# Row fetching in a recommender kernel: SyncE takes a tile of rows every 5.35 steps instead of every 5.5, ScalarE one tile more

## The chip, the cores and the metric

The kernel runs on one core of a Trainium2 chip. The metric is the time on the device in microseconds (us), the median of the timed runs. One further execution is recorded by the hardware profiler; every row of the profile comes from it. The engines are named as the profile names them: PE (TensorE, with its weight loads as PEld), DVE (VectorE), ACT (ScalarE), POOL (GpSimd) and SP (SyncE). ACT and SP also issue transfers on DMA queues of their own, written ACTq and SPq.

## The reference

For each of 16384 examples there are 69 user ids and one label id. Each id picks a row of 96 floats from a table of 100001 rows. Every user row is weighted by a small attention network that sees it beside the label's row; the weighted rows are summed in 10 groups, and a network of three layers follows.

```
u   = emb[batch_user]                       # 16384 x 69 x 96
ql  = emb[batch_label[:, 0]]
z   = concatenate([q, u, q - u, q * u])     # q is ql for all 69
h   = dice(z @ W1 + b1, a1)                 # 64 wide
att = (h @ W2 + b2) @ W3 + b3
pre = where(batch_user < ITEM_NUM, u * att, 0)
pooled = einsum('gf,bfe->bge', window, pre) # 10 groups
x   = concatenate([pooled, ql])
x   = dice(bn(x @ Wf1 + bf1), af1)          # 200 wide
x   = dice(bn(x @ Wf2 + bf2), af2)          # 80 wide
return x @ Wf3 + bf3
```

The bulk of the memory work is the lookup of 16384 x 69 = 1130496 rows of 384 bytes, that is, 8832 tiles of 128 rows. A row is put on each of 128 partitions.

## The kernel before

The examples are cut into 32 blocks of 512. A block has 69 chunks of 512 looked-up rows, and a chunk has four tiles of 128 rows. Two chunks together are a pair, which is the work of one step: 1104 steps (NPAIR) in all, eight tiles each.

Each tile's rows come in one of three ways. Most are gathered by POOL, with one indirect DMA per tile (`gather`, L265 and L266) into a buffer `u` of which there are 15. Some are fetched by SP, row by row: one DMA of 384 bytes for each row, at an address that SP has first loaded into a register (class `Singles`: `load` with L286, `fetch` with L301). The rest are fetched in the same way by ACT. Only the last of the four tiles of a chunk (SLOT = 3) can be fetched row by row. The lists SP_CHUNKS and ACT_CHUNKS (L52, L55) say in which chunks. SP has the odd chunks, so the second chunk of a pair; its tile number s lies in step int(5.5 s) + 6, 199 tiles in all. ACT has even chunks; its tile number s lies in step (s + 1) * 128 // 20 + 2, 170 tiles in all. That leaves 8832 - 199 - 170 = 8463 gathers for POOL, and 128 more for the label rows (`head_gather`).

The rows that SP and ACT fetch land in `ring`, twelve buffers of 128 rows: eight for SP, four for ACT. PE waits on a semaphore before it reads one (`wait_for_single`, L318), and a tile that reuses a buffer waits until PE has finished with the tile that was in it.

In a step PE transposes the eight tiles (`fetch`, L359, through `read_rows`, L325), DVE copies the transposed rows and multiplies them with the label's, PE forms the hidden layer (`hidden`), ACT and DVE apply its activation, PE makes the attention weights (`attend_rows`, `spread`), and seven steps after the fetch (POOL_LAG) PE multiplies the same rows again with the weights to pool them (`pool`, also L325 through `read_rows`). The three layers on top of a finished block (`top1`, `top2`, `top3`) are spread over later steps.

The order on every engine is written out by hand in `plan`, a list of work for each step. SP's tile is planned six steps ahead of its use (L598 and L599); on SP itself there is nothing else but a few loads of ids, one every four blocks (`load_ids`, planned 50 steps ahead of their first use), and the stores of the result at the end. ACT's rows are planned 20 per step (`scalar_rows`, L610), behind the activations of the step, so ACT's queue holds both in one order. Behind the waiting transpose of a fetched tile stands all further work of PE.

Of the kernel before, what the change touches and what calls it, by code (L numbers as in the profile page):

```python
# [18 lines left out]
P = 128  # L19
# [29 lines left out]

ROW_BYTES = 4 * E  # L50
SLOT = 3
SP_CHUNKS = [2 * (int(5.5 * s) + 6) + 1 for s in range(199)]  # L52
SP_RING = 8
ACT_ROWS = 20
ACT_CHUNKS = [2 * ((s + 1) * P // ACT_ROWS + 2) for s in range(170)]  # L55
ACT_RING = 4
SINGLES = SP_CHUNKS + ACT_CHUNKS
NSB = (len(SINGLES) + P - 1) // P
# [57 lines left out]
def rec_kernel(  # L116
# [477 lines left out]
    def at(step, *work):  # L594
        plan.setdefault(step, []).extend(work)

    by_sync = Singles("sp", nc.sync, mybir.EngineType.SP, SP_CHUNKS, 0, range(SP_RING), 32)
    for s, m in enumerate(SP_CHUNKS):  # L598
        at(max(0, m // 2 - 6), lambda s=s: by_sync.fetch(s, 0, P))  # L599
# [4 lines left out]
        mybir.EngineType.Activation,  # L604
        ACT_CHUNKS,
        len(SP_CHUNKS),
        range(SP_RING, SP_RING + ACT_RING),
        32,
    )
    def scalar_rows(i):  # L610

        row, stop = i * ACT_ROWS, min((i + 1) * ACT_ROWS, len(ACT_CHUNKS) * P)
        while row < stop:
# [140 lines left out]
```

## Time and profile before

| | us |
|---|---|
| timed runs, median of 3 (lowest, highest) | 16757.55 (16755.94, 16759.19) |
| the profiled execution's own time | 10782.2 |
| its span, first to last instruction | 10780.4 |
| PE busy, mean granted clock 0.749 | 8756.9 |
| POOL busy | 8110.8 |
| DVE busy | 4235.1 |
| ACT busy | 1884.4 |

The profiled execution is 5975 us shorter than the timed runs. Every row of the profile therefore describes an execution of 10782 us, and what the timed runs do in the rest is not in it.

How to read it: a group's row names the line, the engine, the operation and the tiles (output, then inputs), the count, the busy time in us and the mean of one in ns, and after the second bar the idle time of the engine just before such instructions and what ended it. "issue" means that nothing which the profile shows was waited for. Instructions that only issue a DMA, load a register or wait on a semaphore are not counted as busy: SP, which does nothing else, has no share at all, and ACT's share leaves out its row fetching. In a view of one tile the three numbers of a row are the shortest, median and longest duration in ns, then the first and last start in us.

### The profile page before, as it was taken

What the parts mean: (1) busy time and instruction counts of PE and PEld (TensorE: products, weight loads), DVE (VectorE), ACT (ScalarE), POOL (GpSimd) and SP (SyncE); (2) the same over time, 40 slices, a digit from 0 to 9 for tenths busy, and PEclk for the clock granted to TensorE, in tenths of its full rate; (3) what the DMA queues carried; (4) which work ended last, traced back from release to release, by engine and by line L of the source; (5) the groups of instructions that cost most, each with busy time, mean ns of one, the idle gap of its engine ahead of it and who ended that gap; (6) DMA issues with size and microseconds to landing.
All of it is one profiled execution on the core that took longest, in us unless ns stands there. A gap on an engine that the chain in (4) does not pass through costs nothing.

```text
span 10780.4 us, 204439 instructions
## 1 busy us (share of the span) xinstructions
PE 8756.9 (81%) x41797; PEld 4310.8 (40%) x41797; DVE 4235.1 (39%) x7535; ACT 1884.4 (17%) x2761; POOL 8110.8 (75%) x8597
## 2 busy tenths in 40 slices
PE   6888888888887788877888788888887887888888
PEld 3434444434433344433433344333343343443335
DVE  4333333333333333333333343333333334333333
ACT  1111111111111111111111111111111111111112
POOL 7777777777777777777777777777777777777776
PEclk7777777677777777777777777777777777777778
DMA  2222222222222222222222222222222222222221
GB/s 50 42 42 42 45 42 42 42 42 45 42 42 42 45 42 42 42 42 45 42 42 42 42 44 42 42 42 42 44 42 42 42 42 44 42 42 42 42 42 34
DMA packets 372495, 460.70 MB, mean 43 GB/s; under 512 B 232114, under 2 KB 232626, under 8 KB 371106
## 3 DMA queue, kind: packets, MB, share of 16 engines
q0 software_dynamic: 274912, 422.81, 18.9%
q1 hardware_dynamic: 52802, 16.36, 1.0%
q10 hardware_dynamic: 43520, 8.44, 0.7%
q14 instruction: 925, 7.58, 0.2%
q8 instruction: 336, 5.51, 0.2%
HBM read 446.81 MB, written 0.07 MB: 41 GB/s over the span
## 4 chain that ended last, share of the span: by engine, by line
POOL 40%; PE 21%; issue 19%; DMA 12%; ACTq 6%; ACT 2%; DVE 1%; POOLq 0%
POOL u L266 40%; DMA u<-in_rows,ids 12%; ACTq L301 4%; PE acc L325 4%; PE p L502 4%; PE ph L399 3%; PE ph L403 3%; PE ptr L325 2%; PE prow L414 1%; ACTq L286 1%; PE pa L423 1%; ACT y L405 1%; POOL q L266 1%; PE ph L396 1%; PE ph L401 1%
## 5 line engine op out<-in xcount | busy, mean ns | idle before, releaser
L266 POOL DMA_INDIRECT u<-in_rows,ids x8463 | 7989.1, 944 | 2583.5 <-issue 2389.6
L325 PE MATMUL ptr<-ident,u 128*96 128x128 f32 x8463 | 1925.1, 332 | 1606.1 <-DMA u<-in_rows,ids 1555.6
L407 DVE TENSOR_TENSOR y<-ph,y 128x512 f32<-128x512 f32 x1104 | 763.5, 692 | 4972.6 <-ACT y L406 4699.0
L325 PEld LDWEIGHTS acc<-rw,u 128*96 128x96 f32 x15702 | 1674.4, 188 | 1332.5 <-issue 840.4
L325 PEld LDWEIGHTS ptr<-ident,u 128*96 128x96 f32 x8463 | 1131.6, 151 | 2282.7 <-DMA u<-in_rows,ids 1853.2
L325 PE MATMUL acc<-rw,u 128*96 128x20 f32 x15702 | 1792.0, 259 | 212.0 <-DVE rw L436 177.6
L376 DVE COPY uT<-ptr 96x512 f32<-96x512 f32 x2208 | 1489.0, 674 | 739.9 <-PE ptr L325 737.5
L405 ACT ACTIVATE y<-ph 128x512 f32<-128x512 f32 x1104 | 658.8, 597 | 6119.1 <-PE ph L403 3304.1
L399 PE MATMUL ph<-uT,A 128*64 128x512 f32 x4096 | 1598.9, 856 | 0.0
L403 PE MATMUL ph<-quT,wn 96*64 96x512 f32 x4416 | 1540.5, 767 | 0.0
L379 DVE TENSOR_TENSOR quT<-ptr,qT 96x512 f32<-96x512 f32 x2048 | 1379.1, 673 | 0.0
L406 ACT ACTIVATE y<-y,wn,na1c 128x512 f32<-128x512 f32 x1104 | 897.9, 813 | 36.6
L403 PEld LDWEIGHTS ph<-quT,wn 96*64 96x64 f32 x4416 | 429.4, 183 | 1002.5 <-issue 1001.8
L502 PE MATMUL p<-pooled,wf 96*100 96x512 f32 (+1 forms) x1400 | 667.7, 624 | 0.0
L414 PE MATMUL prow<-y,v 128*32 128x512 f32 x2208 | 507.2, 885 | 65.4 <-DVE y L407 57.6
L399 PEld LDWEIGHTS ph<-uT,A 128*64 128x64 f32 x4096 | 259.6, 172 | 609.6 <-issue 605.5
L416 ACT COPY row<-prow 128x512 f32<-128x512 f32 (+1 forms) x277 | 161.6, 583 | 1733.2 <-issue 675.0
L470 DVE COPY pooled<-acc 96x160 f32<-96x160 f32 x1008 | 420.5, 417 | 99.1 <-PE acc L325 97.6
L502 PE MATMUL p<-pre,V 96*100 96x512 f32 (+1 forms) x700 | 398.0, 714 | 11.1 <-DVE x L485 10.8
L502 PEld LDWEIGHTS p<-pooled,wf 96*100 96x100 f32 x1400 | 249.6, 190 | 316.5 <-issue 316.5
L436 DVE SCALAR_TENSOR_TENSOR rw<-patt,bb,wn 128x320 f32<-128x320 f32 x554 | 276.1, 539 | 116.8 <-PE patt L431 114.7
L485 DVE SCALAR_TENSOR_TENSOR x<-p,wf,g 100x512 f32<-100x512 f32 (+3 forms) x105 | 73.9, 704 | 523.6 <-ACT g L484 523.5
(72 smaller groups left out, 2706.1 us busy)
## 6 DMA issues: line engine op xcount, KB each, us to landing
ring<-in_rows SPq DMA_DIRECT2D x25472, 0.4 KB
ring<-in_rows ACTq DMA_DIRECT2D x21760, 0.4 KB
u<-in_rows,ids POOLq DMA_INDIRECT x8463
ids<-in_idx SPq DMA_DIRECT2D x8, 560.0 KB, 3.9
q<-in_emb,ids POOLq DMA_INDIRECT x128
wf<-in_far SPq DMA_DIRECT2D x1, 1209.0 KB, 8.3
wn<-in_near SPq DMA_DIRECT2D x1, 236.0 KB, 3.4
offsets<-in_single_rows SPq DMA_DIRECT2D x1, 192.0 KB, 2.5
```

What stands on the lines that cost most here:

```text
L266: nc.gpsimd.indirect_dma_start(out=dst, out_offset=None, in_=table, in_offset=bass.IndirectOffsetOnAxis(ap=index, axis=0),)
L301: d = self.engine.dma_start(out=ring[r : r + 1, b], in_=row_bytes[:, bass.ds(self.values[r], ROW_BYTES)]).then_inc(self.sems[k], 16)
L325: ins = op(out, ring[:, at[0]].bitcast(F32) if at else u[:, 4 * (c % 2) + t, :], other, **how)
L376: nc.vector.tensor_copy(uT[j][0:E], ptr)
L379: nc.vector.tensor_tensor(quT[:, j, :].rearrange("e (s f) -> e s f", f=FM), ptr.rearrange("e (s f) -> e s f", f=FM), by_field(q[:, k * NS ...
L399: nc.tensor.matmul(p, As[n % 2][:, k // 4, :], uT[j], start=True, stop=False)
L403: nc.tensor.matmul(p, Wp, quT[:, j, :], start=False, stop=True)
L405: nc.scalar.activation(y, ph, AF.Sigmoid, scale=S_DICE)
L406: nc.scalar.activation(y, y, AF.Identity, bias=a1c, scale=na1c)
L407: nc.vector.tensor_mul(y, ph, y)
L414: nc.tensor.matmul(pr[32 * k : 32 * (k + 1), :], v2, ys[b + k], start=True, stop=True)
L502: nc.tensor.matmul(p1, w[:, h * DH : (h + 1) * DH], x, start=(k == 0), stop=(k == KTOP - 1))
```

## The change

Two numbers change in each of two lists. SP's tile number s now lies in step int(5.35 s) + 6, and there are 204 of them in place of 199. ACT's list keeps its spacing and has one tile more at its end, number 170, in step 1096. What is in these lists is no longer gathered by POOL. The buffers, the lead of six steps, ACT's 20 rows per step and all other work stay as they are.

```diff
-SP_CHUNKS = [2 * (int(5.5 * s) + 6) + 1 for s in range(199)]
+SP_CHUNKS = [2 * (int(5.35 * s) + 6) + 1 for s in range(204)]
 SP_RING = 8
 ACT_ROWS = 20
-ACT_CHUNKS = [2 * ((s + 1) * P // ACT_ROWS + 2) for s in range(170)]
+ACT_CHUNKS = [2 * ((s + 1) * P // ACT_ROWS + 2) for s in range(171)]
 ACT_RING = 4
```

## The prediction

> **What bounds the kernel now.** I read the page first, busy time and chain, because it says whether the engine that the change relieves sets the time.
>
> ```profile
> PE 8756.9 (81%) x41797; PEld 4310.8 (40%) x41797; DVE 4235.1 (39%) x7535; ACT 1884.4 (17%) x2761; POOL 8110.8 (75%) x8597
> POOL u L266 40%; DMA u<-in_rows,ids 12%; ACTq L301 4%; PE acc L325 4%; PE p L502 4%; PE ph L399 3%; PE ph L403 3%; PE ptr L325 2%; PE prow L414 1%; ACTq L286 1%; PE pa L423 1%; ACT y L405 1%; POOL q L266 1%; PE ph L396 1%; PE ph L401 1%
> L266 POOL DMA_INDIRECT u<-in_rows,ids x8463 | 7989.1, 944 | 2583.5 <-issue 2389.6
> ```
>
> PE is busiest by share, yet the chain runs mostly through POOL's gathers (L266), and the idle time ahead of a gather is "issue": nothing was being waited for. So next the timeline of POOL in mid-kernel and at its end, and the gathers' busy time in four equal stretches.
>
> ```profile
> 5002.83 0.94 POOL L266 DMA_INDIRECT u<-in_rows,ids  x1 [0.30 <-issue]
> 5004.08 0.94 POOL L266 DMA_INDIRECT u<-in_rows,ids  x1 [0.30 <-issue]
> ...
> 10733.37 0.94 POOL L266 DMA_INDIRECT u<-in_rows,ids  x1 [0.30 <-issue]
> 10734.61 0.95 POOL L266 DMA_INDIRECT u<-in_rows,ids  x1 [0.30 <-issue]
> ```
>
> ```profile
> 1000.00:3000.00 2000.00, 1511.23 (x1602) 0.74 0.21 43
> 3000.00:5000.00 2000.00, 1511.19 (x1602) 0.75 0.21 43
> 5000.00:7000.00 2000.00, 1510.95 (x1603) 0.76 0.21 43
> 7000.00:9000.00 2000.00, 1511.23 (x1602) 0.75 0.21 43
> ```
>
> The columns are the stretch, its length, POOL's busy time and count, the clock, the DMA share and GB/s. The reader should see one gather every 2000 / 1602 = 1.248 us, alike in all stretches. 8463 gathers of users and 128 of labels make 8591; 8591 x 1.249 = 10730 us, and the first starts at 3.2 us, so the last should end near 10734; it ends at 10735.6. POOL is never held up. The profiled span is those 10736 us and a tail of 45 us.
>
> Two other queues fetch rows one by one. Their limits come from the view of the row buffer (tile ring), the row loads, the waits of SP's queue, and the timelines of SP and PE.
>
> ```profile
> L301 SPq DMA_DIRECT2D ring<-in_rows x25472: 227/228/482, 6.7 to 10349.8; - x199
> L301 ACTq DMA_DIRECT2D ring<-in_rows x21760: 213/214/587, 18.6 to 10606.0; - x200
> L286 SPq TENSOR_LOAD <-offsets x796: 2025/2176/2410, 4.5 to 10337.5; - x199
> ...
> SPq L301 <- PE ptr L325: 84.8, 36, 13.2
> SPq L301 <- PE acc L325: 27.5, 7, 10.9
> SPq L301 <- PE ph L403: 0.9, 4, 0.3
> ...
> 6.74 48.92 SPq L301 DMA_DIRECT2D ring<-in_rows  x128
> 79.65 0.27 PE L325 MATMUL ptr<-ident,ring 128*96 128x128 f32 x1
> 10677.94 0.42 PE L325 MATMUL ptr<-ident,ring 128*96 128x128 f32 x1
> ```
>
> SP is nearly full too. From 6.7 to 10349.8 us it waits only 113 us for a free buffer. Taking off the waits and the 49 us of the last tile leaves (10343.1 - 113.2 - 49) / 198 = 51.4 us per tile. The kernel takes 10780 / 1104 = 9.76 us per step, so 5.5 steps are 53.7 us. SP issues its first tile by 55.7 us and PE reads it at 79.65: a lead of 24 us. The last is issued by 10350 and read at 10678: a lead of 328 us. SP gains about 2 us per tile until the eight buffers stop it; the waits are that stop.
>
> **What the skill's pages say.** Perfetto Trace Analysis, section Identifying the Most-Contended Engine, takes the engine with the highest occupancy, for GPSIMD the occupancy percentage. By it POOL would have a quarter of its time free. The trace disagrees: the 0.30 us after each gather come back every time with no wait behind them. The forecast goes by the period, 1.249 us. DMA: Bandwidth & Descriptors, section Why a DMA increments its semaphore by 16 and not by 1, says that a transfer with one row uses one engine, the lowest-numbered, on SP and ACT alike. All single rows would then share one DMA engine. The profile gives their two queues 1.0% and 0.7% of sixteen engines, at most 27% of one; with 18.9% for the gathers that engine is under half busy, so 768 further rows (1.6% of 47232) should not slow it. The trace does not name the engine.
>
> **The change, part by part.** SP: 204 tiles for 199, so 5 more tiles, 640 more rows, 20 more loads of offsets. ACT: one more tile, 128 rows and 4 loads. POOL: 8463 - 5 - 1 = 8457 gathers. PE, DVE and the ACT activations keep their counts; a transpose or a pooling product reads the ring instead of a gathered tile (239 ns for either, in the groups of pooling products).
>
> POOL, on the path: 6 x 1.249 = 7.5 us less. The tail after the last gather is PE's chain and keeps its 45 us.
>
> SP, off the path: five tiles are 5 x 51.4 = 257 us more issuing, hidden while the lead is positive. One tile per 5.35 steps is needed every 5.35 x 9.76 = 52.2 us against 51.4: a margin of 0.8 us, where it was 2.3. The dangerous place is the start. Tile 2 moves from step 17 to step 16, whose fourth transposes begin at 176.4 us before the change, and SP is done with it at 55.7 + 2 x 51.3 = 158.3: a lead of 18 us. The landing takes about 1 us more. Step by step with the old step times this is the smallest lead. The last tile, 203, is at step 1092; SP finishes it near 55.7 + 203 x 51.4 = 10490 us and PE wants it near 10646, 156 us later. With such leads SP never reaches the buffer limit, so the 113 us of waits should vanish; those waits cost nothing now. The ids loads, queued between tiles on SP, are planned 50 steps (some 490 us) ahead and stay early. If the cover fails, PE stands before its transpose (wait_for_single), and behind it stand all later PE work, the release of gather buffers and then POOL: each us short per tile costs about a us per tile.
>
> ACT, on the path only near the end: its 20 rows per step and the loads stay as they were, but go on for 6.4 steps longer, steps 1088 to 1094, with the tile read at step 1096. That is 128 x 0.32 + 4 x 2.27 = 50 us of ACT's queue, the 0.32 us being the spacing of rows that are not held up (20 in 6.37 us at 5016 us), in steps of 62 us that also hold activations of the last blocks. ACT does this all through the kernel with POOL unhindered. Bounds: nothing while POOL's 15 buffers absorb it, 50 us if all of it were exposed; I take nothing. No gain can come from it. A ring read instead of a gathered one could spare PE some of its 3488 us of waiting on gathers, but PE does not set the end; bounded by 0 and the 7.5 us that POOL grants.
>
> Sum against the profiled execution: 10782.2 - 7.5 = 10774.7 us, -0.07%.
>
> **Against the median.** The timed runs are 16757.55 us, 5975 us longer than the profiled execution, and no view shows where. They spread by 3 us in 16757, so whatever adds it is as regular as POOL's gathers. If the gathers set those runs too, a period is (16757.5 - 48) / 8591 = 1.945 us and six are 11.7 us; if the excess is something apart, the gain stays 7.5 us. I take the first, an estimate: 16757.6 - 11.7 = 16745.9. Both are within 0.2%, about what a measurement of this kernel can tell from no change.
>
> **The rivals.**
> No gain: in the timed runs PE or the excess sets the time and POOL has slack. For it: PE is busy 81%, and its clock is 0.75. Against: the profile's unbroken row of gathers. 16757.
> SP becomes the limit (slower). Its place is the wait before the ring transpose; it decides when a tile costs SP more than 5.35 steps. In the profile that needs 0.8 us more per tile. In the timed runs a step is 16757.55 / 1104 = 15.18 us: if the excess sits in the rows that SP issues, a tile takes 5.5 x 15.18 = 83.5 us, five more are 418 us, and three more steps follow the last tile, 3 x 9.76 = 29 us: 17204. For it: SP is the second fullest resource, and one step period fits as well as another. Against: rows are issued here with leads up to 328 us.
> A smaller loss: rows share a DMA engine or ACT's last tile shows. 768 rows beside 47232 + 8591 x 8 rows on one engine are +0.6%, 16860 if that engine sets the timed runs; ACT's tile gives at most 50 us, some 78 us at 15.18 us per step: 16824. Against: the queues' low shares.
> Faster: the timed runs hold a disturbance that a different spacing of SP's rows removes in part; then anywhere from 16700 down to the profile's 10775. Nothing in the trace speaks for it but the gap itself.
>
> **How the numbers follow.** The likeliest, gathers set the pace, 0.62 (its own range 16725 to 16775); no gain 0.08; smaller loss 0.08; SP the limit 0.15; faster by over 0.2% 0.07. Same is 0.62 + 0.08 = 0.70, slower 0.23, faster 0.07. The range reaches from 16690, taking in the small gains, to 16870, taking in the smaller losses; it leaves out SP as the limit and the large gains, about 0.19.
>
> **What would show it.** 8457 gathers of users at 944 ns with 0.30 us of issue between them, some 1602 per 2000 us; a span near 10773; SP with 26112 rows, hardly a wait for PE, its last row near 10490 us; PE reading SP's last tile about 150 us later; ACT's rows ending some 60 us later than 10606. I am wrong if PE waits ahead of ring transposes, gaps open between POOL's gathers, SP's tile takes over 52 us, or the timed runs move where the profile does not: then the excess of 5975 us lies in the rows and not in the gathers.

## The result and the profile after

The changed kernel takes 17020.54 us (median of 4 runs, 17013.28 to 17026.13), the kernel before 16758.37: 1.57% slower, ratio 1.0157 with a 95% interval of 1.0145 to 1.0169. The forecast was 16746, within 16690 to 16870.

On two of the four chips that the experiments met, the kernel before takes some 16760 us every time, and on the other two some 10782 us every time. (One of the long chips was met on two occasions, the other three on one each.) The one profile that the prediction had was of the second sort, and all its timed runs were of the first. Below these are called the long chips and the short chips, and only runs of the same sort are compared.

The page of the changed kernel's profile, on a long chip: the busy line, the chain, and the groups of gathers and of ring transposes.

```profile
PE 8944.0 (53%) x41797; PEld 4580.1 (27%) x41797; DVE 4209.5 (25%) x7535; ACT 1882.8 (11%) x2761; POOL 8101.4 (48%) x8591
SPq 62%; issue 36%; PE 1%; ACTq 0%; DMA 0%; ACT 0%; DVE 0%; POOL 0%; another core or an unknown queue 0%
SPq L301 54%; SPq L286 8%; ACTq L301 0%; PE p L502 0%; PE acc L325 0%; DMA ring<-in_rows 0%; PE ph L399 0%; PE ptr L325 0%; PE ph L403 0%; PE patt L431 0%; POOL u L266 0%; ACTq L286 0%; ACT y L405 0%; PE prow L414 0%
L266 POOL DMA_INDIRECT u<-in_rows,ids x8457 | 7979.6, 944 | 8774.5 <-PE ptr L325 3354.8
L325 PE MATMUL ptr<-ident,ring 128*96 128x128 f32 x375 | 139.4, 372 | 4411.4 <-DMA ring<-in_rows 4343.0
```

A gather still takes 944 ns and POOL's work is the same, but POOL now stands idle for 8774.5 us. The chain is SP's queue from end to end: 62% for SP's instructions and 36% for the time between them in which nothing was waited for. PE waits 4343 us for rows that SP fetches (the idle time in the last row). No engine's share of busy time would have pointed there, as SP has none.

The gathers in four stretches of the changed kernel (columns as in the prediction: 1602 per stretch had been the full row), and SP's timeline over some 100 us, of the changed kernel and of the first profile of the kernel before, on a short chip:

```profile
1000.00:3000.00 2000.00, 947.31 (x1004) 0.67 0.14 27
3000.00:5000.00 2000.00, 960.51 (x1018) 0.67 0.14 27
5000.00:7000.00 2000.00, 966.12 (x1024) 0.67 0.14 27
7000.00:9000.00 2000.00, 947.33 (x1004) 0.68 0.14 27
```

```profile
5000.18 99.74 SPq L301 DMA_DIRECT2D ring<-in_rows  x161
3999.88 109.75 SPq L301 DMA_DIRECT2D ring<-in_rows  x277
```

The changed kernel's SP issues 161 rows in 99.74 us, 0.62 us a row. In the first profile of the kernel before it issued 277 in 109.75 us, 0.40 us a row. SP does not wait for a free buffer meanwhile: in its own list of waits nothing but 1.4 us is left under L301. It just issues more slowly.

### The profile page after: what moved, and what is told of

It reads as the page before. It is cut to its first block, busy times and chain, and to the rows that moved or that the text cites. A ratio compares the mean times of both kernels' runs of the same rounds, so it can differ in the third digit from the quotient of the medians.

```text
span 17013.7 us, 205998 instructions
## 1 busy us (share of the span) xinstructions
PE 8944.0 (53%) x41797; PEld 4580.1 (27%) x41797; DVE 4209.5 (25%) x7535; ACT 1882.8 (11%) x2761; POOL 8101.4 (48%) x8591
## 4 chain that ended last, share of the span: by engine, by line
SPq 62%; issue 36%; PE 1%; ACTq 0%; DMA 0%; ACT 0%; DVE 0%; POOL 0%; another core or an unknown queue 0%
SPq L301 54%; SPq L286 8%; ACTq L301 0%; PE p L502 0%; PE acc L325 0%; DMA ring<-in_rows 0%; PE ph L399 0%; PE ptr L325 0%; PE ph L403 0%; PE patt L431 0%; POOL u L266 0%; ACTq L286 0%; ACT y L405 0%; PE prow L414 0%
## 5 line engine op out<-in xcount | busy, mean ns | idle before, releaser
L266 POOL DMA_INDIRECT u<-in_rows,ids x8457 | 7979.6, 944 | 8774.5 <-PE ptr L325 3354.8
L325 PE MATMUL acc<-rw,u 128*96 128x20 f32 x15688 | 1915.1, 268 | 1155.8 <-issue 491.4
L325 PE MATMUL ptr<-ident,ring 128*96 128x128 f32 x375 | 139.4, 372 | 4411.4 <-DMA ring<-in_rows 4343.0
L325 PEld LDWEIGHTS acc<-rw,u 128*96 128x96 f32 x15688 | 1795.3, 199 | 2268.1 <-issue 1296.3
L325 PE MATMUL ptr<-ident,u 128*96 128x128 f32 x8457 | 1518.8, 330 | 451.9 <-issue 358.5
L325 PEld LDWEIGHTS ptr<-ident,u 128*96 128x96 f32 x8457 | 1188.1, 161 | 605.3 <-issue 528.5
L325 PEld LDWEIGHTS ptr<-ident,ring 128*96 128x96 f32 x375 | 56.9, 152 | 4476.2 <-issue 4044.8
L414 PE MATMUL prow<-y,v 128*32 128x512 f32 x2208 | 704.4, 861 | 903.9 <-issue 518.6
L502 PE MATMUL p<-pooled,wf 96*100 96x512 f32 (+1 forms) x1400 | 714.6, 650 | 62.5 <-issue 61.1
L431 PE MATMUL patt<-ident,row 128*128 128x128 f32 x1108 | 236.6, 351 | 352.9 <-issue 148.5
```

Of the source, the lines that this page charges most:

```text
L266: nc.gpsimd.indirect_dma_start(out=dst, out_offset=None, in_=table, in_offset=bass.IndirectOffsetOnAxis(ap=index, axis=0),)
L325: ins = op(out, ring[:, at[0]].bitcast(F32) if at else u[:, 4 * (c % 2) + t, :], other, **how)
L414: nc.tensor.matmul(pr[32 * k : 32 * (k + 1), :], v2, ys[b + k], start=True, stop=True)
L502: nc.tensor.matmul(p1, w[:, h * DH : (h + 1) * DH], x, start=(k == 0), stop=(k == KTOP - 1))
```

## The experiments

Each kernel is the kernel before with the edit shown. Four theories stood at one time or another. Theory A: SP's queue alone sets the end. Theory B: the rows of SP and ACT together do, at 0.3548 us each (the ratio of rows, 48000 / 47232 = 1.0163, is close to the ratio of times). Theory C: POOL's gathers slow the issue of rows. Theory D: the rows are slow by themselves, or by what PE and ACT issue. The forecast's own theory, that gathers set the pace, is the rival of all four.

**The kernel before once more, for a profile on a long chip.** No edit.

> The kernel before, unchanged, to get a profile of the slow kind of execution. If its timed runs and the one profile of 10782 us are two kinds of execution, this profile should have a span near 16757 us, with gaps between POOL's gathers, PE waiting ahead of ring transposes and SP's tile taking 5.5 x 15.2 = 83 us. If the profile always runs at 10782 us and only unprofiled runs are slow, it has 10782 again.

It took 16758.7 us, with a span of 16757.0. From its page, its waits and SP's timeline:

```profile
L266 POOL DMA_INDIRECT u<-in_rows,ids x8463 | 7985.9, 944 | 8506.5 <-PE ptr L325 2912.9
PE ptr L325 <- DMA ring<-in_rows: 4063.5, 185, 48.8
5000.08 99.71 SPq L301 DMA_DIRECT2D ring<-in_rows  x160
```

So the kernel before is set by SP too on a long chip: POOL idle for 8506 us, PE waiting 4063 us for rows, 0.62 us a row. The change met a kernel that already waited for the queue which it lengthens. The profile also gives the rate by POOL's state. Call a stretch in which POOL's gathers follow one another without a wait a burst. Counted in the trace, SP issues 12279 rows inside bursts, in 10405 us, 0.85 us a row with the loads of offsets, and 13193 rows outside, in 6222 us, 0.47 us a row. In the first profile, on a short chip, SP took 0.41 us a row with POOL gathering all the time (25472 rows in 10343 us).

**The two parts apart.** The change is three numbers, two in SP's list and one in ACT's.

```diff
-SP_CHUNKS = [2 * (int(5.5 * s) + 6) + 1 for s in range(199)]
+SP_CHUNKS = [2 * (int(5.35 * s) + 6) + 1 for s in range(204)]
```

> Only SP's part of the change: 204 tiles, ACT's list as before. Theory A, SP's queue alone sets the end: the whole loss is there, 17020 us (+1.6%). Theory B, the single rows of SP and ACT together set the end at 16757 / 47232 = 0.3548 us a row: 640 rows more, 16757 + 227 = 16984 us (+1.35%). If gathers set the pace: 16757 - 5 x 1.9 = 16748.

```diff
-ACT_CHUNKS = [2 * ((s + 1) * P // ACT_ROWS + 2) for s in range(170)]
+ACT_CHUNKS = [2 * ((s + 1) * P // ACT_ROWS + 2) for s in range(171)]
```

> Only ACT's part: one more tile at the end of its list. Theory A: unchanged, 16757 us (0 to +50). Theory B: 128 rows at 0.3548 us, +45 us, 16803 us (+0.27%). If gathers set the pace: 16755.

On one long chip: SP's part 16995.2 us against 16764.6, ratio 1.0129 (1.0112 to 1.0146); ACT's part 16773.4, ratio 1.0007 (0.9999 to 1.0016). SP's part carries most of the loss: 231 us for five tiles, 46 us a tile and 0.36 us a row. It lies below theory A's figure (17020) and within reach of theory B's (16984). ACT's part can't be told from no change, which is against theory B (1.0027). The two parts add up to 240 us, the whole change to 262, which these intervals allow.

**No rows on ACT.**

```diff
-ACT_CHUNKS = [2 * ((s + 1) * P // ACT_ROWS + 2) for s in range(170)]
+ACT_CHUNKS = [2 * ((s + 1) * P // ACT_ROWS + 2) for s in range(0)]
```

> ACT fetches no rows; SP's 199 tiles stay, POOL gathers 170 tiles more (8633 and 128). Theory A: SP still needs 84 us a tile, 16750 us. Theory B: 25472 rows at 0.3548 are 9037 us, less than POOL's 8761 x 1.249 + 48 = 10990 us, which then sets the time.

15753.7 us on the same chip, near neither figure. Taking away 21760 rows of ACT freed 1011 us, so ACT's rows do slow SP's, but they are not the cause: B is out, and A lacks the slowing. In this trace SP takes 0.72 us a row beside gathers and 0.47 with POOL still. The gathers are what both traces have in common.

**No gathers.** This kernel leaves out the gathers of user rows; PE reads one constant tile in their place:

```diff
-        u = upool.tile([P, 8, E], F32, tag="u", name=f"u{i}")
+        u = still
...
-                    gather(rows, u[:, 4 * j + t, :], ids[n][:, 4 * k + t : 4 * k + t + 1])
+                    pass
...
+    still = const.tile([P, 8, E], F32, name="still")
+    nc.vector.memset(still, 0.01)
```

> Leaves out the gathers of user rows: PE reads one constant tile in place of each gathered one, while SP's 199 and ACT's 170 tiles are fetched and read as before. Theory C, POOL's gathers slow the issue of single rows (0.85 us a row on SP with POOL busy, 0.47 with POOL idle, in the profile of the kernel before in the slow execution): SP returns to some 0.40 us a row, 51 us a tile, and the span is 10200 to 10700 us. Theory D, SP's rows are slow by themselves or by PE's and ACT's instructions: SP's tile stays near 83 us and the span near 16700.

10397.0 us, on a chip where the kernel before takes 16766. SP's timeline and the page's chain:

```profile
5001.53 61.39 SPq L301 DMA_DIRECT2D ring<-in_rows  x160
SPq L301 45%; ACTq L301 11%; SPq L286 11%; ACTq L286 3%; PE p L505 2%; ACT y L408 2%; PE acc L325 1%; PE ph L402 1%; PE ph L406 1%; PE ptr L325 1%; PE prow L417 1%; ACT y L409 1%; DMA ring<-in_rows 0%; PE pa L426 0%; PE ph L399 0%
```

160 rows in 61.39 us, 0.38 us a row: without gathers SP is as quick on a long chip as on a short one, with the same PE, DVE and ACT work beside it. Theory D is out. This was also as far as SP can go: 199 x 51.4 = 10229 us.

**Rows left out on SP, and on both.**

```diff
-SP_CHUNKS = [2 * (int(5.5 * s) + 6) + 1 for s in range(199)]
+SP_CHUNKS = [2 * (int(5.5 * s) + 6) + 1 for s in range(0)]
```

> SP fetches no rows; ACT's 170 tiles stay. Theory C: ACT's rows are slowed as SP's were: at 0.7 us a row while POOL gathers (SP's figure without ACT's rows) ACT issues 15300 of its 21760 rows in POOL's 10.98 ms and needs 3 ms more: 13500 to 14500 us. If only SP suffers: POOL sets the end, 8790 x 1.249 + 48 = 11027 us.

14137.0 us, inside the first range: ACT's rows are slowed as SP's are.

With both lists empty (and NSB held at 1, so that the tile of offsets exists):

> No single rows at all: POOL gathers all 8832 tiles and the 128 of labels. All theories: POOL without a pause, 8960 x 1.249 + 48 = 11240 us, a third less than before.

13488.6 us, ratio 0.8043 (0.802 to 0.8066). This is the best version that was found for a long chip, and yet the expectation of 11240 us failed by 2249. There are no single rows, and POOL is still idle for 4873 us. PE's timeline in this run shows a part of why, at the matmuls of one head (L348), 32 alike that need nothing new from anyone:

```profile
5012.94 0.31 PE L348 MATMUL pc<-Cq,qT 97*32 97x64 f32 x1
5014.07 0.27 PE L348 MATMUL pc<-Cq,qT 97*32 97x64 f32 x1 [0.82 <-issue]
5015.48 0.30 PE L348 MATMUL pc<-Cq,qT 97*32 97x64 f32 x1 [1.14 <-issue]
5016.89 0.27 PE L348 MATMUL pc<-Cq,qT 97*32 97x64 f32 x1 [1.10 <-issue]
5018.30 0.42 PE L348 MATMUL pc<-Cq,qT 97*32 97x64 f32 x2 [1.15 <-issue]
5019.73 2.72 PE L348 MATMUL pc<-Cq,qT 97*32 97x64 f32 x24 [1.00 <-issue]
```

PE gets one matmul off in 1.1 to 1.4 us; then 24 follow in 2.72 us, 0.11 us each. POOL's timeline has a gather every 1.25 us up to 5015.74, which ends at 5016.69, and the next at 5020.14. The quick ones begin only 3 us after the last gather has ended, and go on beside the first two of the next burst. So not rows alone are slow: PE's issue is as well, and its slowness comes and goes a little later than the gathers do.

**A tile per 10 steps on SP, none on ACT.**

```diff
-SP_CHUNKS = [2 * (int(5.5 * s) + 6) + 1 for s in range(199)]
+SP_CHUNKS = [2 * (10 * s + 6) + 1 for s in range(109)]
-ACT_CHUNKS = [2 * ((s + 1) * P // ACT_ROWS + 2) for s in range(170)]
+ACT_CHUNKS = [2 * ((s + 1) * P // ACT_ROWS + 2) for s in range(0)]
```

> SP fetches a tile per 10 steps (109 tiles), ACT none. Theory C: at 0.72 us a row with POOL busy a tile takes SP 92 us plus the loads' share, less than 10 steps of 10.05 us, so PE never waits for SP and POOL sets the end: 8851 x 1.249 + 48 = 11103 us, 1.2% under the kernel that only gathers. If SP's rows cost more beside an unbroken row of gathers (over 0.79 us), it is slower than that kernel.

13542.6 us, ratio 0.8068 (0.8046 to 0.8091): no better than gathers alone. The expectation failed as the one before it did, since POOL does not run unbroken in either.

**Four kernels that met a short chip.** A tile per 6 steps on SP (182 tiles), the descriptor space of the gathers doubled (RING_BYTES 8192), and two kernels in which the gathers are made but not awaited: PE reads the constant tile, as above, and the gathers go to tiles that nobody reads.

```diff
+        u, g = still, upool.tile([P, 8, E], F32, tag="u", name=f"u{i}")
...
+                    gather(rows, g[0:P, 4 * j + t, :], ids[n][0:P, 4 * k + t : 4 * k + t + 1])
```

The fourth has 16 in place of P in that line.

> SP fetches a tile per 6 steps, 182 in place of 199; ACT as before. If a tile more or less costs SP's undisturbed issuing time, because the time that it adds or frees is time in which POOL stands still: 17 x 51.4 = 874 us less, and some 10 us for 17 gathers more: 15900 us (0.949). If it costs the mean spacing of tiles, 84 us: 17 x 84 = 1428 us less, 15340 us (0.915). If SP is no longer the limit after the first few tiles: less gain than 874.

> All gathers are made as before, but PE reads one constant tile in place of what they bring (the single rows are read as before). Theory C: the gathers alone, awaited by nobody, slow SP: span 15800 to 16800 us. If SP was slow because PE, held by gathers, frees its buffers late: 10400 us, as without gathers.

> As the run with unread gathers, but each gather brings 16 rows in place of 128 (an eighth of the data; the rest is left out). If it is the gathered rows and their descriptors that slow the issue on SP: close to the 10400 us without gathers (under 11500). If it is POOL's instruction for each gather, whatever it moves: near the run with unread gathers.

> The kernel before with 8192 bytes in place of 4096 for the descriptors of POOL's gathers. If the rows are slowed because that space is short: faster by hundreds of us (under 16000). Otherwise unchanged, 16757 us.

The kernel before took 10781.6 us here in 23 runs, so none of these figures speaks to the theories of long chips. Measured: 182 tiles 10799.1 us, ratio 1.0017 (1.001 to 1.0024), which is POOL's price for 17 gathers more, 17 x 1.249 = 21 us, give or take the tail; unread gathers 10742.0; 16 rows per gather 10417.7; doubled descriptor space 10775.5, no difference that one run can show. A second run of the 182 tiles met a short chip again: 10801.3 us, 1.0017.

> 182 tiles on SP in place of 199, one per 6 steps. Where the kernel before takes 16758 us: a tile's worth is SP's issuing time with POOL standing still, 46 us (5 tiles cost 231 in the run with SP's part alone) to 60 us (128 rows at 0.47), so 780 to 1025 us less, 15730 to 15980 us; if it is the mean spacing of 84 us, 15330 us. Where the kernel before takes 10782 us: 10799 as in its first run.

**The same two with unread gathers, on a long chip.**

> All gathers made but PE reads one constant tile in their place. Where the kernel before takes 10782 us: 10742 us as in its first run. Where it takes 16758 us, theory C (gathers slow the issue of instructions): 15800 to 16800 us; if SP was slow because PE, held by gathers, frees buffers late: 10740 us.

> The same with 16 rows per gather in place of 128. Where the kernel before takes 10782 us: 10418 us as in its first run. Where it takes 16758 us: under 11500 if the gathered rows and their descriptors slow the issue; near the run with full unread gathers if it is POOL's instruction for each gather, whatever it moves.

20842.7 and 20884.2 us, where the kernel before took 16778.9. That is theory C, and far beyond the range that it gave: nobody waits for these gathers, so POOL's bursts last 67 us at the median where they last 9.7 in the kernel before, and beside them SP, ACT and PE nearly stop. The busy table of the run with full gathers, for a stretch with POOL gathering and one with POOL still (PE, PEld, DVE, ACT and POOL, each busy us and count, then clock, DMA share, GB/s), and SP's timeline in the same stretches:

```profile
2700.00:3000.00 300.00, 55.91 (x144) 24.75 (x144) 13.53 (x23) 7.60 (x11) 229.63 (x230) 0.51 0.19 38
2150.00:2600.00 450.00, 350.63 (x1756) 176.65 (x1758) 180.22 (x324) 79.15 (x116) 0.00 (x0) 0.79 0.02 3
```

```profile
2701.91 297.75 SPq L301 DMA_DIRECT2D ring<-in_rows  x105
2150.02 449.93 SPq L301 DMA_DIRECT2D ring<-in_rows  x1124
```

105 rows in 298 us beside gathers, 2.8 us each; 1124 in 450 us without, 0.40 us. PE: 144 matmuls in 300 us against 1756 in 450. Over the whole trace a register move of SP, which transfers nothing, takes 643 ns on average beside gathers and 39 ns with POOL still. The run with 16 rows per gather, an eighth of the data, has the same two stretches:

```profile
2700.00:3000.00 300.00, 56.13 (x144) 24.76 (x144) 13.53 (x23) 7.60 (x11) 229.00 (x227) 0.50 0.04 5
2700.78 296.32 SPq L301 DMA_DIRECT2D ring<-in_rows  x105
```

5 GB/s in place of 38, and the same 105 rows and 144 matmuls. So it is not the bytes that gathers bring. The pages of the two profiles add a limit to that reading: the gathers' queue counts 274912 packets in both, 32 for each gather, only smaller ones. Whether the gather instruction, its descriptors or these packets slow the issue is not told apart.

Nor is it the gather only while it runs. Here are the last gather before a pause of POOL and the first after it, in the run with full gathers, then SP's rows early in the pause and a little later:

```profile
3396.89 0.94 POOL L266 DMA_INDIRECT u<-in_rows,ids  x1 [0.30 <-issue]
3691.35 0.94 POOL L266 DMA_INDIRECT q<-in_emb,ids  x1 [293.52 <-PE pq L339]
```

```profile
3399.63 21.00 SPq L301 DMA_DIRECT2D ring<-in_rows  x8
3428.03 22.05 SPq L301 DMA_DIRECT2D ring<-in_rows  x60
```

The last gather ends at 3397.8 us and its packets by 3399.1, yet SP issues 8 rows in the next 21 us, as slowly as before, and only then 60 in 22 us. All 30 pauses of over 30 us in this trace are alike: SP is quick again 23 to 28 us after the last gather, and 24 to 29 us in the run with 16 rows. After the short bursts of the kernel before (five to ten gathers) it takes about 1 us. It reads as if the gathers left something behind that has to be worked off, and a long burst more of it; no view names it.

The bytes also answer the shared DMA engine, which the prediction weighed with the Trainium skill: the share of the gathers' queue falls from 10.2% to 1.9% of sixteen engines, and nothing changed. The Trainium skill's page DMA: Bandwidth & Descriptors, section SWDGE vs HWDGE vs iDMA, holds transfers issued from SP and ACT immune to one interference, VectorE's lock on POOL's descriptor rings. What these runs show is another one: these rows are not immune to the gathers, and neither are moves and matmuls.

**The changed kernel and gathers only, again.**

> The changed kernel again. Executions of one program come in two kinds, and the kernel before tells which one a chip gives. Where it takes 10782 us, gathers set the end and the changed kernel takes 6 x 1.249 = 7.5 us less, ratio 0.9993 (0.999 to 1.000). Where it takes 16758 us, SP sets the end and the changed kernel takes 17020 us, ratio 1.0157.

> No single rows. Where the kernel before takes 10782 us: 8960 x 1.249 + 48 = 11240 us, ratio 1.042, so that there the single rows pay for themselves. Where it takes 16758 us: 13490 us, ratio 0.804, as in its first run.

Both on a long chip: 17021.9 us, ratio 1.0159 (1.0142 to 1.0176), and 13447.1 us, ratio 0.8015 (0.8001 to 0.803). Gathers only was not run on a short chip; there POOL's period gives 8960 x 1.249 + 48 = 11240 us, an estimate, 4% more than the kernel before. Only on the long chips is it measured to beat both kernels.

**The changed kernel on a short chip.**

> The changed kernel once more, for a chip on which the kernel before takes 10782 us: 10774.5 us there, ratio 0.9993. On the others 17020 us, ratio 1.0157, as twice before.

10788.4 us against 10781.5, ratio 1.0008 (1.0000 to 1.0017): not the 7.5 us less of the forecast but about 7 us more, at the edge of no change. The profile shows both the gain and what ate it. First POOL's last gather, then two of PE's rows with the wait ahead of the second, and ACT's queue at that place:

```profile
10727.90 0.94 POOL L266 DMA_INDIRECT u<-in_rows,ids  x1 [0.30 <-issue]
```

```profile
10615.81 1.04 PE L502 MATMUL p<-pooled,wf 96*100 96x128 f32 x8
10628.01 2.45 PE L502 MATMUL p<-pre,V 96*100 96x128 f32 x10 [11.17 <-DVE x L485]
```

```profile
10610.52 8.86 ACTq L301 DMA_DIRECT2D ring<-in_rows  x20
10619.42 0.59 ACT L416 COPY row<-prow 128x512 f32<-128x512 f32 x1 [8.15 <-issue]
10619.90 0.60 ACT L405 ACTIVATE y<-ph 128x512 f32<-128x512 f32 x1
10620.54 0.81 ACT L406 ACTIVATE y<-y,wn,na1c 128x512 f32<-128x512 f32 x1
10620.60 6.03 ACTq L301 DMA_DIRECT2D ring<-in_rows  x20
10626.68 0.37 ACT L483 ACTIVATE g<-p,dice 100x128 f32<-100x128 f32 x1 [5.33 <-issue]
```

The last gather ends at 10728.8 us where it ended at 10735.6: 6.7 us earlier, and SP's leads are close to the forecast (17 us at least, 151 at the last tile). But the tail after it grew from 44.9 to 57.2 us. ACT's additional tile puts 20 rows of 6.03 us between the activation at 10620.54 and the gate g of the top layer (L483). Before the change there are no rows there and g follows at once:

```profile
10620.86 0.81 ACT L406 ACTIVATE y<-y,wn,na1c 128x512 f32<-128x512 f32 x1
10622.11 0.37 ACT L483 ACTIVATE g<-p,dice 100x128 f32<-100x128 f32 x1 [0.43 <-PE p L502]
...
10625.10 1.39 PE L502 MATMUL p<-pre,V 96*100 96x128 f32 x10 [3.03 <-DVE x L485]
```

PE needs what DVE makes of g, and its wait is 11.17 us in place of 3.03. Two steps on, and to the end, PE's transposes are 5.4 to 5.6 us later than before the change, having been 5 to 7 us earlier. The longer wait is 8.1 us of that swing of some 11; the rest was not followed. This is read from one trace of each kernel; ACT's part alone was not run on a short chip.

## Why the prediction was wrong

**The bound.** The step that failed is the first: "POOL is never held up" is true of the execution it was read from, and the timed runs are of another kind. The 5975 us between them were named and then put on the gathers, as a period of 1.945 us. On the long chips a gather takes 944 ns as ever, and POOL stands idle for 8506 us, where it was 2584 in the first profile. The 5975 us are slow issue that comes with the gathers, of SP's rows above all: SP becomes the limit, PE waits 4063 us for its rows, and POOL waits in turn. Three of the prediction's own signs of being wrong came true: PE waiting ahead of ring transposes, gaps between POOL's gathers, and a tile of SP over 52 us (82.6 in the changed kernel).

**The likeliest case, 16746.** Right in none of its terms on the long chips. On a short chip, its 7.5 us showed at POOL's last gather (6.7) and were lost in the tail.

**SP as the limit.** This rival, at 0.15, is what happened, in the place that it named (the wait ahead of the ring transpose). The range left it out. Its size was off: it gave 17204, 447 us more, of which 418 are five tiles at the mean spacing of 83.5 us and 29 are three more steps behind the last tile. Measured are 231 us for SP's part alone and 262 for the whole change. The term that was mis-sized is the price of one more tile. SP's rows in the long-chip profiles of the kernel before and the changed kernel, with first and last start:

```profile
L301 SPq DMA_DIRECT2D ring<-in_rows x25472: 1/228/1469, 7.3 to 16633.6; - x199
L301 SPq DMA_DIRECT2D ring<-in_rows x26112: 1/228/1476, 6.8 to 16848.1; - x200
```

The last row comes 214 us later, 43 us for each of five tiles (191 us later in the second profile of the changed kernel). The counts by POOL's state say why it is so little. Inside bursts SP issues nearly as many rows as before, 12319 for 12279, and the bursts are 10.4 ms in both. The other 600 further rows are issued outside, where SP has 250 us more for them: 0.42 us each, near the undisturbed 0.40. What follows SP's last row grows from 123 to 166 us, where the rival had 29 more; with SP's part alone it is 147. So it is partly luck that five undisturbed tiles, 5 x 51.4 = 257, come so near the whole loss. The reverse, fewer tiles on a long chip, was tried twice and met short chips both times.

**ACT's tile.** Taken as nothing, with 50 us as the upper end. On the short chip the tail is about 12 us longer; on the long chip its part alone is 1.0007, within noise. As far as the one trace shows, the forecast's mistake was to ask whether ACT keeps up, as it does all through the kernel, and not what is queued behind its rows in these last steps: the gates of the last block, which had found an empty queue.

**SP's leads, the vanishing waits for buffers, POOL's period** were right on the short chip: SP waits about 7 us there under L301 where it waited 113, which saved nothing, as said. **No gain** was right in one half, that POOL has slack in the timed runs, and wrong in its number. **Faster** did not occur. The smaller loss by a shared DMA engine, 16860, is the wrong mechanism: an eighth of the data changed nothing.

**What stays open.** Why gathers slow the issue on SP, ACT and PE on some chips and not on others, and what it is that goes on for some 25 us after a long burst. The traces show it in steps of about 0.7 us per instruction, moves included, from 8 us after the start; in them no wait and no transfer was found that would account for it. Doubling the descriptor space was only tried where there is nothing to cure. The recording itself is an untested rival: the timed runs, too, are on record with the core's span and clock, and none shows the kernel's time without that.

## What to carry to other kernels

When the profiled execution and the timed runs differ by a third, the profile is of another bound, and no sum in it may be scaled up to the runs: first get a profile with the runs' time. A queue that only issues DMAs has no busy share, so look at who waits for it and at its rows per us. And where work is moved between two engines of which one slows the other, the mean spacing of the units (83.5 us here) is not the price of one more (some 40): ask in which stretches it will really be issued, and what comes behind the last one.

## What the runs showed of the hardware

On two of four chips indirect gathers on POOL, whether they bring 128 rows or 16, slow the issue of instructions on SP, ACT and PE: register moves of SP take 643 against 39 ns, rows of SP 2.8 against 0.40 us, and matmuls come one per 2.1 us (144 in 300) against one per 0.26. After a long burst this lasts 23 to 28 us beyond the last gather, whose packets are over within 2 us. On the other two chips the same program shows no trace of it: 0.41 us a row and 29 ns a move with POOL gathering without a pause. The difference for the kernel before is 16760 against 10782 us. The best kernel measured on the one sort, gathers only at 13447 to 13489 us, would by the estimate above be 4% slower than the kernel before on the other.
